# Dealing the first period's work by hand, and spreading two rows' statistics over the tail

## The chip, the cores and the metric

One core of a Trainium2 chip runs the whole program. The metric is the device time of one execution in microseconds (us), median over several executions on the chip. The core has five engines that run side by side, each through its own instructions in order: TensorE (PE in the profile; PEld is its weight load), VectorE (DVE), ScalarE (ACT), GpSimd (POOL) and SyncE (SP, which issues most transfers here).

## The reference, cut to what matters

Two graph layers over 32 batches of 512 nodes with 512 features in float32, each followed by a residual sum and a layer norm. Layer 0 adds over the neighbours. Layer 1 is attention with 8 heads, masked by the same adjacency.

```python
# layer 0:  out = deg * (x @ Wi.T + b) + adj @ (x @ Wj.T)
x = layernorm(x + layer0(x, adj, W, b))
# layer 1:  q, k, v from x; scores masked where adj == 0; softmax; @ v; @ Wo.T + bo
x = layernorm(x + layer1(x, adj, Wq, bq, Wk, bk, Wv, bv, Wo, bo))
```

## The kernel before: the parts that matter here

The batches form a software pipeline. Period n does the attention of batch n-1, and between its matmuls the rest of layer 0 and the projections of batch n, the output projection of batch n-2, and the start of batch n+1. A list of small jobs (`todo`) is dealt to eight steps by estimated cost. The loop takes the steps two at a time, so a period is four double steps, and each of them begins with attention work:

```python
for step in range(0, STEPS, size):            # size 2, in the last period 1
    g, kc = divmod(step, NC)
    for i in range(2):
        scores(b, 2 * g + i, kc)              # PE, then the exponentials on ACT, in place
    for f in due:
        values(*f)                            # PE: the double step before
    for i in range(2):
        mask(2 * g + i, kc)                   # DVE: exponentials times edges
    todo = [f for todo in PERIODS[n][step:step + size] for f in todo]
    while todo and todo[0][1] is between:
        run(todo.pop(0))                      # jobs put between masks and next scores
    ...                                       # row sums of a finished group
    for i in range(2):
        scores(b, 2 * g + i, kc + 1)          # needs the buffers that the masks have read
    ...
    for f in todo: ...                        # the other jobs, masks and sums of kc + 1 among them
```

A layer norm is four kinds of job. `stats` takes two rows of 128 nodes each (a "half"):

```python
def ln_stats(mv, y):
    nc.vector.bn_stats(st, y); nc.vector.bn_aggr(mv[:, 0:2], st)           # DVE
    nc.gpsimd.tensor_scalar(...); nc.gpsimd.tensor_tensor(..., OP.pow); nc.gpsimd.tensor_scalar(...)  # POOL, 128x1
def ln_apply(mv, y):
    nc.scalar.activation(y, y, AF.Identity, bias=mv[:, 4:5], scale=mv[:, 3:4])  # ACT
def l0_norm(b, ic, bank=None):
    ...  # four PE transposes of the applied row into PSUM, ACT copies the result to HT
```

In the first period with attention (n = 1) the jobs stand in this order: six layer-0 pieces with the statistics of half 1 before the last of them, apply half 1, statistics and apply of half 0, two transposed blocks, then query, key and value pieces, then the start of batch 2.

```python
for n in range(1, B):
    todo = phase_b(n) + phase_c(n) + phase_a(n + 1)
    if n < B - 1:
        half = sum(f[0] for f in todo) / 2
    PERIODS += [by_steps(todo, half)]         # cuts by cost: statistics cost 0.0
```

## Time and profile before

| what | us | where it is read |
|---|---|---|
| time, median of the first three runs | 3657.97 | the runs |
| span of the profiled run | 3656.2 | page |
| TensorE busy | 3625.8 | page, part 1 |
| TensorE idle in period 1 | 9.4 | busy time by stretch |
| TensorE's clock in period 1's second double step | 0.85 | the same |

The kernel is bound by TensorE at 99%. A reader should ask where the other 30 us are, since a change of order can win only these and what matmuls lose at a lowered clock. Nearly ten of them are in one period of thirty-two. Here are TensorE's largest waits from 100 us on, summed by kind (total, times, longest), four of eight lines; the prediction shows them in place.

```profile
PE mmb L362 <- ACT xh L305: 5.2, 1, 5.2
PE sc L490 <- DVE e L499: 2.4, 2, 1.7
PE mma L362 <- ACT xh L305: 1.8, 1, 1.8
PE mmb L436 <- DVE k L474: 1.5, 1, 1.5
```

L362 is the transposed block, L305 the apply, L490 the scores, L499 the mask, L436 a matmul of a projection, L474 an addition that moves a projection's result out of PSUM (the memory, in banks, that matmuls write to; a bank is free again when its result has been moved out, which is called its evacuation here). A releaser called "issue" means that the profile shows nothing that was waited for. The first and third line are the second double step, the fourth is the last one; the 1.7 of the second line is in the tail.

### The profile page before, as it was taken

How to read it: one execution, taken by the hardware profiler on the slowest of the kernel's cores; microseconds unless marked ns; L12 is line 12 of the kernel's file. 1: busy time of each engine (PE TensorE's matmuls, PEld its weight loads, DVE VectorE, ACT ScalarE, POOL GpSimd, SP SyncE). 2: the span in 40 equal slices, each digit the busy share in tenths (PEclk: the TensorE clock that was granted, in tenths of full speed). 3: DMA queues.
4: the chain of work that ended last, by engine and by line, in shares of the span. 5: the costliest groups of instructions: out<-in, count | busy, mean ns of one | idle time of the engine just before them, and what ended most of it. 6: DMA issues, size and time to landing. Idle time of an engine off the chain costs nothing.

```text
span 3656.2 us, 49768 instructions
## 1 busy us (share of the span) xinstructions
PE 3625.8 (99%) x18470; PEld 2527.7 (69%) x18470; DVE 2369.8 (65%) x3133; ACT 1035.5 (28%) x1485; POOL 2003.7 (55%) x1984
## 2 busy tenths in 40 slices
PE   9999999999999999999999999999999999999998
PEld 6676777677767766776677667767776777677763
DVE  4566766666666666666666566666666766666665
ACT  2222322222322223222222232232222322222322
POOL 3456455565556565465655555654656456565543
PEclk9999999999999999999999999999999999999999
DMA  8344555545554555555455545555455555445541
GB/s 259 119 127 138 145 161 149 134 140 144 160 159 124 143 145 145 165 148 132 135 149 157 159 121 147 145 153 159 138 140 138 147 162 153 130 137 147 160 133 53
DMA packets 797174, 530.02 MB, mean 145 GB/s; under 512 B 530432, under 2 KB 611840, under 8 KB 796928
## 3 DMA queue, kind: packets, MB, share of 16 engines
q1 hardware_dynamic: 780384, 494.78, 49.1%
q10 hardware_dynamic: 16320, 31.46, 2.5%
q8 instruction: 150, 2.46, 0.3%
q14 instruction: 96, 0.79, 0.1%
q0 software_dynamic: 224, 0.53, 0.0%
HBM read 453.25 MB, written 73.40 MB: 144 GB/s over the span
## 4 chain that ended last, share of the span: by engine, by line
PE 97%; DVE 1%; POOL 1%; issue 0%; ACT 0%; DMA 0%; SPq 0%; DVEq 0%; POOLq 0%
PE mma L436 31%; PE mmb L436 31%; PE sc L490 13%; PE ov L516 12%; PE mmb L334 4%; PE mma L334 3%; PE sc L526 2%; PE mmb L607 0%; PE mma L607 0%; DVE e L499 0%; POOL es L505 0%; DVE es L507 0%; DVE rl L535 0%; PE sc L735 0%; DMA big<-in_adj_dram 0%
## 5 line engine op out<-in xcount | busy, mean ns | idle before, releaser
L499 DVE TENSOR_TENSOR e<-sc,edge 128x1024 f32<-128x1024 f32 x512 | 607.5, 1217 | 493.2 <-PE ov L516 479.6
L494 ACT ACTIVATE sc<-sc 128x1024 f32<-128x1024 f32 x512 | 495.3, 1007 | 922.7 <-PE sc L490 920.2
L436 PE MATMUL mmb<-ring,big 128*128 128x256 f32 x3144 | 730.0, 381 | 0.0
L436 PE MATMUL mma<-ring,big 128*128 128x256 f32 x3112 | 721.3, 380 | 0.7 <-DVE v L465 0.7
L436 PEld LDWEIGHTS mmb<-ring,big 128*128 128x128 f32 x3144 | 595.9, 190 | 104.2 <-issue 24.3
L436 PEld LDWEIGHTS mma<-ring,big 128*128 128x128 f32 x3112 | 588.4, 190 | 105.3 <-issue 22.5
L405 POOL TENSOR_TENSOR big<-big 128x512 f32<-128x512 f32 x376 | 489.1, 1326 | 258.0 <-PE sc L490 234.4
L490 PE MATMUL sc<-q,k 64*128 64x512 f32 x2048 | 513.9, 620 | 2.5 <-DVE e L499 2.4
L516 PE MATMUL ov<-e,v 128*32 128x512 f32 x4096 | 466.8, 595 | 1.2 <-DVE oT L544 1.2
L204 POOL TENSOR_TENSOR xlo<-xh,xhi 128x512 fp32r<-128x512 f32 x128 | 162.2, 1278 | 526.8 <-ACT xhi L203 526.8
L436 PE MATMUL mma<-big,ring 128*128 128x256 f32 x1808 | 429.3, 380 | 0.8 <-issue 0.8
L436 PE MATMUL mmb<-big,ring 128*128 128x256 f32 x1776 | 421.3, 380 | 1.5 <-DVE k L474 1.5
L436 PEld LDWEIGHTS mma<-big,ring 128*128 128x128 f32 x1808 | 342.1, 190 | 62.0 <-issue 14.1
L436 PEld LDWEIGHTS mmb<-big,ring 128*128 128x128 f32 x1776 | 335.6, 190 | 60.9 <-issue 12.2
L490 PEld LDWEIGHTS sc<-q,k 64*128 64x128 f32 x2048 | 165.5, 185 | 287.7 <-DVE e L499 145.8
L300 POOL TENSOR_SCALAR mv<-mv 128x1 f32<-128x1 f32 x256 | 79.8, 312 | 512.4 <-DVE mv L299 500.0
L516 PEld LDWEIGHTS ov<-e,v 128*32 128x32 f32 x4096 | 119.8, 109 | 328.5 <-issue 325.3
L505 POOL TENSOR_TENSOR es<-e 128x1024 f32<-128x1024 f32 x128 | 300.0, 2355 | 77.4 <-DVE e L499 77.4
L507 DVE TENSOR_TENSOR es<-es,e 128x1024 f32<-128x1024 f32 x250 | 300.7, 1224 | 0.0
L451 POOL TENSOR_TENSOR xh<-xh,p 128x512 f32<-128x512 f32 x186 | 230.6, 1268 | 110.3 <-ACT p L443 110.3
L349 POOL TENSOR_TENSOR big<-big,deg_r 128x512 f32<-128x512 f32 x124 | 212.1, 1710 | 76.4 <-DVE big L348 76.4
L454 DVE TENSOR_TENSOR xh<-xh,mma 128x512 f32<-128x512 f32 x186 | 126.9, 682 | 191.2 <-PE mma L436 174.6
(163 smaller groups left out, 3544.0 us busy)
## 6 DMA issues: line engine op xcount, KB each, us to landing
ring<-wo SPq DMA_DIRECT2D x217, 256.0 KB, 2.9
ring<-wq SPq DMA_DIRECT2D x160, 256.0 KB, 3.7
ring<-wv SPq DMA_DIRECT2D x160, 256.0 KB, 3.2
ring<-wk SPq DMA_DIRECT2D x160, 256.0 KB, 4.4
ring<-wi SPq DMA_DIRECT2D x155, 256.0 KB, 2.6
ring<-wj SPq DMA_DIRECT2D x155, 256.0 KB, 2.6
xh<-in_x_dram SPq DMA_DIRECT2D x32, 1024.0 KB, 6.2
xa<-in_x_dram SPq DMA_DIRECT2D x124, 256.0 KB, 4.3
```

The costliest lines, as they stand in the source:

```text
L204: nc.gpsimd.tensor_sub(lo, xs, hi.bitcast(FT))
L334: nc.tensor.matmul(pm, parts[w][:, jc, :], adjR[:, jc, :], start=(w == 0 and jc == 0), stop=(w == 1 and jc == NC - 1))
L349: nc.gpsimd.tensor_tensor(XD[b][:, dc, :], XD[b][:, dc, :], deg_r, op=OP.mult)
L405: nc.gpsimd.tensor_tensor(dst, p, q, op=OP.subtract)
L436: nc.tensor.matmul(pm[:, c * Q:(c + 1) * Q], lhs, rhs, start=first, stop=(kc == 1 and n == len(terms) - 1), skip_group_check=True)
L451: nc.gpsimd.tensor_tensor(d, d, p1, op=OP.add)
L490: nc.tensor.matmul(ps[:, s, :], KT[b, hp // 2][r, hp % 2, kc * P:(kc + 1) * P], QT[b, hp // 2][r, hp % 2, :], start=True, stop=True)
L494: nc.scalar.activation(ps, ps, AF.Exp, scale=QSCALE)
L499: nc.vector.tensor_tensor(e, ps, edge[:, kc:kc + 1, :].to_broadcast([P, 2, N]), op=OP.mult)
L505: nc.gpsimd.tensor_add(ES[i], E[i, 0], E[i, 1])
L507: nc.vector.tensor_add(ES[i], ES[i], E[i, kc])
L516: nc.tensor.matmul(PV[g][r][32 * h:32 * h + 32, :], V[b][:, kc, c0:c0 + 32], E[h // 2, kc][:, h % 2, :], start=(kc == 0), stop=(kc == NC - 1))
```

## The change

The intent: in period 1 the four cuts are set by hand. Layer 0 with all its statistics and applies goes to the first double step, the transposed blocks and the first-half pieces to the second, the rest of the projections to the third, the start of batch 2 to the fourth. In the tail, the statistics of batch 30's four rows are taken two in one step and two in the next.

```diff
@@ last_steps
-                [p[3]], [p[4]], [own[0], z(stats, m, 0), z(stats, m, 1)], [own[1], z(apply, m, 0), z(apply, m, 1), z(store, m)], []]
+                [p[3]], [p[4]], [own[0], z(stats, m, 0)], [own[1], z(apply, m, 0), z(stats, m, 1)], [z(apply, m, 1), z(store, m)]]
@@ for n in range(1, B):
+        if n == 1:
+            a, b, c = [todo.index(f) for f in ((TR, l0_norm, 1, 0, banks(1)[0]), pc("k", 1, 2, banks(1)[0]), phase_a(2)[0])]
+            PERIODS += [[todo[:a], [], todo[a:b], [], todo[b:c], [], todo[c:], []]]
+            continue
```

## The prediction

> **What bounds the kernel now.** I read the page first (busy shares, slices), then PE's waits, then the timelines of the two stretches that the diff touches, then busy time by stretch.
>
> ```profile
> PE 3625.8 (99%) x18470; PEld 2527.7 (69%) x18470; DVE 2369.8 (65%) x3133; ACT 1035.5 (28%) x1485; POOL 2003.7 (55%) x1984
> ```
>
> TensorE is busy 3625.8 of 3656.2 us, so 30.4 us is all the idle time there is. The change adds and removes no matmul: it can win only that idle time, and what matmuls lose at a lower clock. The start (no matmul before 4.04 us, small gaps after) and the end (last matmul at 3649.0, program end at 3656.2) hold about half of it, and neither is touched. The rest lies in period 1 (106.49 to 217.13 us: attention of batch 0, projections of batch 1, start of batch 2) and in the tail. By stretch (length, then PE busy; the clock follows POOL's column), the four double steps of period 1, and then period 2, which is the steady state:
>
> ```profile
> 106.49:131.44 24.95, 24.95 (x114) 19.46 (x113) 10.66 (x15) 3.85 (x4) 20.29 (x19) 1.00 0.42 123
> 131.44:164.86 33.42, 26.39 (x129) 18.11 (x129) 15.16 (x20) 12.94 (x20) 9.40 (x12) 0.85 0.31 95
> 164.86:191.84 26.98, 26.13 (x138) 17.51 (x137) 16.19 (x22) 6.82 (x10) 7.58 (x5) 1.00 0.69 185
> 191.84:217.13 25.29, 23.80 (x121) 15.69 (x121) 20.86 (x22) 6.71 (x9) 13.59 (x10) 1.00 0.25 75
> 217.13:329.30 112.17, 112.17 (x577) 78.95 (x576) 73.73 (x97) 32.10 (x46) 63.01 (x63) 1.00 0.52 146
> ```
>
> Period 2 has no idle time at all, so whatever period 1 saves moves everything after it earlier. The second double step has 7.03 us idle and a mean clock of 0.85: (1 - 0.85) / (1 - 0.5) x 33.42, some 10 us at half rate. The timeline of it:
>
> ```profile
> 136.92 2.03 PE L490 MATMUL sc<-q,k 64*128 64x512 f32 x8
> 144.16 1.12 PE L362 MATMUL mmb<-ident,xh 128*128 128x128 f32 x4 [5.21 <-ACT xh L305]
> 147.10 1.12 PE L362 MATMUL mma<-ident,xh 128*128 128x128 f32 x4 [1.83 <-ACT xh L305]
> 148.01 3.62 PE L436 MATMUL mmb<-ring,big 128*128 128x256 f32 x8
> ...
> 177.74 1.97 PE L436 MATMUL mma<-big,ring 128*128 128x256 f32 x8 [0.85 <-issue]
> ...
> 210.03 1.99 PE L436 MATMUL mmb<-big,ring 128*128 128x256 f32 x8 [1.49 <-DVE k L474]
> ```
>
> The transposes of batch 1 wait for the normalised rows; afterwards eight matmuls take 3.62 us that take 1.89 elsewhere. Why the rows are late is on VectorE:
>
> ```profile
> 137.69 2.35 DVE L507 TENSOR_TENSOR es<-es,e 128x1024 f32<-128x1024 f32 x2
> 139.95 1.21 DVE L499 TENSOR_TENSOR e<-sc,edge 128x1024 f32<-128x1024 f32 x1
> 141.09 0.68 DVE L298 BATCH_NORM_STATS2 st<-xh 128x6 f32<-128x512 f32 x1
> ```
>
> The sum of the last layer-0 piece was done at 132.3, but the statistics of half 0 were dealt to the second double step, behind two masks, two sums of exponentials and a third mask: 8.8 us later.
>
> **What the Trainium skill says.** (1) "TensorE: Matmul & The Clock Gate", Part 1: the array runs at half clock after an idle window of about 3.4 us and needs a busy one to recover; the windows run freely. The trace agrees: the 5.21 us gap is followed by about 10 us at half rate, while gaps of 1.49 and 1.69 us are not. (2) The same page, "Architectural detail": ScalarE's and VectorE's queues are strict FIFO. The trace agrees: the two applies of half 1, ready at 132.3 (GpSimd's last operation for them), ran at 139.92, behind four exponentials. (3) "SBUF — State Buffer", "Who interferes with whom": a VectorE instruction with two SBUF inputs and a GpSimd one that reads SBUF exclude each other. The trace agrees: a 0.26 us GpSimd scalar operation took 1.94 at 144.26, beside a sum of exponentials on VectorE. This is why the second row came 2.95 us after the first.
>
> **The change, part by part: period 1.** The loop takes steps in pairs, so the four non-empty lists are the four double steps. The order of pieces is kept; only the cuts move.
>
> Stage 1 keeps its six layer-0 pieces, 24.95 us, and gains at its end apply (half 1), statistics and apply (half 0). VectorE starts the latter at 132.2 instead of 141.09 and ends 1.7 later, at 133.9; GpSimd makes three small operations a row (1.2 us), ending at 134.4 and 135.65; ScalarE applies the rows (0.8 each), ending at 135.2 and 136.5.
>
> Stage 2 then has scores, values, scores (7.44 us: 191.84 to 199.28 is the same), four transposed blocks (1.74; eight transposes took 0.87 at 155.19), five pieces (8.7, at 1.73 each): 17.9 us. Two waits are new. The first exponentials now stand behind the applies: 136.45 instead of 132.61. The first ends at 137.45, its mask (1.22) at 138.7, and only then may the next scores reuse that buffer; PE would have been ready at 136.92. That is 1.8, and 0.1 for the second buffer. The transposes follow at 140.8 with no wait, but their copies on ScalarE (0.56) stand behind the next two exponentials, which end at 142.0; the first value piece starts at about 142.55 instead of 141.7: 0.85. Stage 2 is 17.9 + 1.95 + 0.85 = 20.7 us.
>
> Stage 3: scores, values, row sums, scores (8.31, as 164.86 to 173.17) and eleven pieces (19.1): 27.4. The 0.85 "issue" of before is, by my reading, a bank wait: the evacuation that frees it stood behind four reciprocals and two products (VectorE 172.09 to 176.86). Now the last first-half key piece, evacuated by ScalarE, stands in front. The reciprocals end about 12.0 after the stage's start; the first query evacuation ends at 12.9, and the piece that needs it is due at 13.5: no wait.
>
> Stage 4 becomes exactly what it is in period 2, 302.22 to 329.32: 27.10 us, no idle time. The 1.49 disappears with the shifted cut.
>
> Sum: 24.95 + 20.7 + 27.4 + 27.1 = 100.15 against 110.64: 10.5. I take 10.3, as neither new wait can be trusted to a tenth.
>
> **The tail.** Matmul, VectorE and GpSimd:
>
> ```profile
> 3627.23 1.13 PE L490 MATMUL sc<-q,k 64*128 64x512 f32 x4 [1.69 <-DVE e L499]
> ...
> 3625.95 2.36 DVE L499 TENSOR_TENSOR e<-sc,edge 128x1024 f32<-128x1024 f32 x2 [3.72 <-POOL es L505]
> ...
> 3622.43 0.19 POOL L300 TENSOR_SCALAR mv<-mv 128x1 f32<-128x1 f32 x1
> 3622.70 0.55 POOL L301 TENSOR_TENSOR mv<-mv,mhalf 128x1 f32<-128x1 f32 x1
> 3623.36 0.26 POOL L302 TENSOR_SCALAR mv<-mv 128x1 f32<-128x1 f32 x1
> 3623.58 2.34 POOL L505 TENSOR_TENSOR es<-e 128x1024 f32<-128x1024 f32 x1
> ```
>
> Scores waited for a mask, the mask for a buffer that a GpSimd sum reads, and that sum stood behind the small operations of four rows. Two rows move a step later: 2 x 1.27 = 2.5 us off this chain. The sum ends at 3623.4, the mask at 3624.7, and PE needs the buffer at 3625.4: the whole 1.69 goes, plus 0.2 of restart, 1.9. The moved statistics run at 3624.7 to 3626.3 on VectorE, before the next mask can start (its exponential ends at 3626.6). The moved applies lie behind the last exponentials, and end about 3629.2, before ScalarE's row-sum drain, due 3632.6. The store goes out 4.5 us later, still over 20 us before the end. I count 1.8.
>
> Together 12.1: 3657.97 - 12.1 = 3645.9.
>
> **Rivals.** *The clock falls again.* The waits of 1.8 and 0.85 lie 4 us apart with transposes between; if they count as an idle window, the half rate returns and costs about what it did: 10.3 lost in that stage less 7.04 idle is 3.3. For: the windows' thresholds are not in the trace. Against: gaps of 1.69 left the clock alone. It makes 3649. *The exponentials behind the applies cost more than I say*, or the evacuations in stage 3 block: 1 to 3 us, 3647 to 3649. For: ScalarE's and VectorE's queues are in order, and more is now put in front of them. *The gain is hidden anyway*, because weight loads or layer-0 input for batch 2 now arrive late: 3656. Against: the ring is seven tiles deep with 3 us loads, and batch 2's first use is now about 17 us after its load is issued, instead of 11. *The tail gains nothing*, if another operand holds the mask: 3648.
>
> **Range and chances.** Repeats of before span 2.1 us. The best case is both new waits overlapped, 3643; the rivals that I believe end at 3649 to 3650. So 3643 to 3650 at 8 in 10. A 2% change is 73 us, over twice all idle time, and nothing here can lose as much: within 2% at 0.98.
>
> **What would show it.** Right: no lowered clock between 106 and 217 us; period 1 about 100 us; the 5.21 and 1.83 us waits replaced by one near 1.8 us of the scores for a mask and one under 1 us of the value piece for the transposed copy; no wait in stages 3 and 4; in the tail no wait over a microsecond for a mask. Wrong: a half-rate stretch still there, a new wait over 3 us in stage 2 or 3, or a mask still released by GpSimd's sum.

## The result, and the profile after

The change takes 3646.07 us (3644.95 to 3648.8, six runs) against 3658.1 (3657.25 to 3659.63, six runs). The ratio is 0.9968, with an interval of 0.9955 to 0.998. A ratio here is the mean time of one kernel's fast runs over that of the other's of the same rounds, so it is not quite the ratio of the medians. Run a second time in a later experiment, beside another set of runs of before, the change had 3646.33 us and 0.997.

In the profile taken with these runs TensorE is busy for 3624.8 us, 1.0 less than before:

```profile
PE 3624.8 (99%) x18470; PEld 2526.2 (69%) x18470; DVE 2370.0 (65%) x3133; ACT 1036.1 (28%) x1485; POOL 2004.7 (55%) x1984
```

The four double steps of period 1 in that profile (length, then busy time of PE, PEld, DVE, ACT, POOL; then the granted clock):

```profile
108.68:133.63 24.95, 24.95 (x113) 19.45 (x113) 10.67 (x15) 4.24 (x5) 20.31 (x19) 1.00 0.42 125
133.63:155.82 22.19, 20.05 (x105) 12.15 (x104) 14.41 (x18) 11.09 (x16) 5.33 (x11) 0.92 0.25 68
155.82:183.32 27.50, 27.50 (x145) 19.12 (x144) 16.48 (x23) 7.39 (x12) 9.61 (x6) 1.00 0.70 204
183.32:210.43 27.11, 27.11 (x138) 18.80 (x137) 20.93 (x23) 7.82 (x11) 14.03 (x10) 1.00 0.44 111
```

The first, third and fourth are as the prediction has them, full to the end. The second has 2.1 us idle, and its clock is 0.92, not 1: the fall that the prediction hoped to be rid of is shorter, but there. In the second profile of the change (the later experiment) the other three have the same lengths, and this one differs:

```profile
131.26:152.39 21.13, 18.61 (x105) 11.45 (x104) 14.41 (x18) 11.01 (x16) 5.33 (x11) 1.00 0.23 67
```

The clock stayed, and the stretch is 1.06 us shorter. TensorE's timeline there, first in the first profile, then in the second (start, length, instruction, and in brackets the idle time before it):

```profile
141.12 3.21 PE L490 MATMUL sc<-q,k 64*128 64x512 f32 x8 [1.93 <-DVE e L499]
144.26 1.11 PE L362 MATMUL mmb<-ident,xh 128*128 128x128 f32 x4
```

```profile
138.75 2.26 PE L490 MATMUL sc<-q,k 64*128 64x512 f32 x8 [1.93 <-DVE e L499]
140.94 0.65 PE L362 MATMUL mmb<-ident,xh 128*128 128x128 f32 x4
141.43 0.60 PE L362 MATMUL mma<-ident,xh 128*128 128x128 f32 x4
142.62 1.99 PE L436 MATMUL mmb<-ring,big 128*128 128x256 f32 x8 [0.59 <-ACT big L363]
```

Both have the same new wait of 1.93 us. In the first, the scores after it take 3.21 us, in the second 2.26. The second also shows the other new wait, 0.59 us of the first value piece for the copy (L363).

In the tail, the scores of the last step start without a wait: the sum on GpSimd stands behind two rows, not four, and the mask that it releases is early enough. PE, DVE and POOL in the first profile:

```profile
3617.52 1.99 PE L490 MATMUL sc<-q,k 64*128 64x512 f32 x8
...
3616.58 1.23 DVE L499 TENSOR_TENSOR e<-sc,edge 128x1024 f32<-128x1024 f32 x1 [1.24 <-POOL es L505]
...
3614.16 2.38 POOL L505 TENSOR_TENSOR es<-e 128x1024 f32<-128x1024 f32 x1
```

The account, before against the second profile of the change (spans 3656.16 and 3644.10 us):

| part | before | change | difference |
|---|---|---|---|
| start to the first scores | 106.49 | 106.31 | -0.2 |
| period 1 | 110.64 | 100.69 | -9.95 |
| periods 2 to 31 | 3352.1 | 3352.0 | -0.1 |
| period 32 and tail, to the start of the last matmul | 79.49 | 77.53 | -1.96 |
| start of the last matmul to the end | 7.4 | 7.5 | +0.1 |

The gain is not idle time alone. TensorE's busy time is 3625.8 us before and 3622.3 in this profile, so 3.5 of the 12.06 us between the spans are matmul time. In period 1 the busy time fell by 3.1 us (101.27 to 98.17, the sums over the four double steps) and the idle time by 6.85 (9.37 to 2.52). That fits the clock, as an estimate: before, TensorE worked for 6.06 of the 10.24 us at half rate, which loses half of that, 3.0 us.

In the first profile the start took 108.68 us, 2.2 more, in code that the change doesn't touch; it is the slowest of its six runs (3648.8). The trace shows both parts of it. The first transposes waited 6.8 us for the adjacency, in the second profile 5.5. And TensorE was busy 1.07 us longer up to the first scores: the first clock record at full rate is at 19.0 us, in the second profile at 15.4, and four matmuls that began at 17.34 took 1.86 us where four like them take 1.08 later. With the window at half rate (1.44 us of busy time) this is why the page above hides the gain in busy time.

### The profile page after: what moved, and what is told of

Same layout as the page of the kernel before. It is cut to its first block, busy times and chain, and to the rows that moved or that the text cites.

```text
span 3647.0 us, 49766 instructions
## 1 busy us (share of the span) xinstructions
PE 3624.8 (99%) x18470; PEld 2526.2 (69%) x18470; DVE 2370.0 (65%) x3133; ACT 1036.1 (28%) x1485; POOL 2004.7 (55%) x1984
## 4 chain that ended last, share of the span: by engine, by line
PE 98%; DVE 1%; POOL 0%; ACT 0%; DMA 0%; issue 0%; SPq 0%; DVEq 0%; POOLq 0%
PE mma L436 31%; PE mmb L436 31%; PE sc L490 13%; PE ov L516 12%; PE mmb L334 4%; PE mma L334 3%; PE sc L526 2%; PE mmb L607 0%; PE mma L607 0%; DVE rl L535 0%; DMA big<-in_adj_dram 0%; PE sc L735 0%; DVE e L499 0%; POOL es L505 0%; POOL big L405 0%
## 5 line engine op out<-in xcount | busy, mean ns | idle before, releaser
L436 PEld LDWEIGHTS mma<-big,ring 128*128 128x128 f32 x1808 | 341.7, 190 | 60.0 <-issue 12.1
L454 DVE TENSOR_TENSOR xh<-xh,mmb 128x512 f32<-128x512 f32 x186 | 127.0, 683 | 190.6 <-PE mmb L436 174.2
```

The lines of the kernel that those rows point to most:

```text
L436: nc.tensor.matmul(pm[:, c * Q:(c + 1) * Q], lhs, rhs, start=first, stop=(kc == 1 and n == len(terms) - 1), skip_group_check=True)
L454: nc.vector.tensor_tensor(d, d, pm, op=OP.add)
```

## The experiments

Ten variants and the change once more ran, each with five timed rounds and beside the kernel before; all were correct. Intervals of the ratios are about 0.0013 to either side, 5 us, so for the small parts the lengths of stretches in the traces carry the verdict, one profile each.

**Period 1 alone** (the change, with the tail of before).

```diff
-                ... [own[0], z(stats, m, 0)], [own[1], z(apply, m, 0), z(stats, m, 1)], [z(apply, m, 1), z(store, m)]]
+                ... [own[0], z(stats, m, 0), z(stats, m, 1)], [own[1], z(apply, m, 0), z(apply, m, 1), z(store, m)], []]
```

> The change's deal of period 1 with the tail of the kernel before. My theory: the two parts add up, period 1 wins about 10 us and the tail about 2, so this run is near 3648 us (3646.5 to 3649.5), ratio to before 0.9973. In its profile the tail's 1.69 us wait of the scores for a mask is back. Rival: part of the gain of period 1 comes only together with the tail, or the tail is worth 3 us or more: then this run is at 3649.5 or above. It also gives one more sample of the clock in period 1: the profile of the whole change showed one stretch of 3.4 us at half rate there; if that depends on where the free-running window falls, it may be missing here, and period 1 then takes about 100 us instead of 101.75.

Measured: 3649.36 us (3647.34 to 3649.72) against 3658.3, ratio 0.9976. Period 1 took 100.69 us, the clock stayed, and in the tail the wait of 1.71 us is back. As expected, at the upper edge.

**The tail alone** (before, with the change's tail; the same lines the other way round).

> The change's tail with the period 1 of the kernel before. Theory: the 1.69 us wait of the scores for the mask goes, and with its restart the tail is 1.9 us shorter: 3656.2 us, ratio 0.9995. Rival: the wait is hidden behind something else at the end (row sums, store), and the time stays at 3658.1; or the traces' difference of the tail, 2.3 us, is all real, 3655.8.

Measured: 3656.8 us (3656.6 to 3657.69) against 3658.3, ratio 0.9997 with an interval that holds 1. In the trace the wait is gone and the stretch from the last period's start to the last matmul is 77.52 us, before 79.49: 1.97 us. The first theory's size is right; that the 2.3 us of the first pair of traces is all real falls, as the rest lies after the last matmul, where the two profiles of the change differ by 0.4 us. The medians of the two parts, 8.9 and 1.5 us, add to 10.4 of some 12. By the traces, 9.95 and 1.97 add to 11.9. The times alone can't tell these apart.

**Only the first cut.**

```diff
+            half = sum(f[0] for f in todo) / 2
+            was = by_steps(todo, half)
+            b, c = [sum(len(s) for s in was[:i]) for i in (4, 6)]
             PERIODS += [[todo[:a], [], todo[a:b], [], todo[b:c], [], todo[c:], []]]
```

(and the tail of before)

> Only the first cut of period 1 is moved (statistics and applies of half 0 go to the end of the first double step); the two later cuts fall where the kernel before has them, and the tail is that of before. Theory: the second double step loses its 5.21 and 1.83 us waits and about 10 us at half rate, and gains a wait near 1.9: about 7.5 us gained. The waits of the third and fourth double step (0.85 and 1.49, with their restarts 2.6) stay, so this is some 2.5 us above the run of period 1 alone: about 3650.5 us. Rival: those two waits were only followers of the late second double step and vanish with it; then this equals the run of period 1 alone, and the hand-made later cuts are worth nothing.

Measured: 3652.31 us (3649.41 to 3653.07), ratio 0.9981; 2.95 us above period 1 alone by the medians, expected 2.5. The times of the two overlap (the lowest here are 3649.41 and 3649.59, the highest there is 3649.72), so the trace decides. TensorE's waits in period 1, the three longest:

```profile
PE sc L490 <- DVE e L499: 1.9, 1, 1.9
PE mmb L436 <- DVE k L474: 1.5, 1, 1.5
PE mma L436 <- issue: 0.9, 1, 0.9
```

The two later waits are exactly where they were, so they belong to the later cuts and did not follow from the late second double step. Which of the two cuts removes which wait was not separated. The third and fourth double step take 26.98 and 25.31 us, as in the kernel before. In this profile the clock fell for one window of 3.4 us, as in the first profile of the change; period 1 took 104.85 us, 3.1 above that one's 101.75.

**The gap filled with useless work** (before, plus matmuls into the bank that the block overwrites).

```diff
         pt = mm_tile(bank) if bank else turn_tile()
+        if b == 1 and ic == 0:
+            for i in range(18):
+                nc.tensor.matmul(pt, adjR[:, 0, 0:P], adjR[:, i % NC, :], start=True, stop=True)
```

> The kernel before, with 18 useless matmuls (0.23 us each, 4.2 us) in front of the first transposed block of batch 1, into the bank that the block then overwrites: they fill most of the 5.21 us in which TensorE waits. They take nothing away from what it waits for. Theory: the idle window is what halves the clock; filled, the clock stays whole, the transposes and the first value piece run at full rate, and the kernel gets about 3 us FASTER for doing more work: 3655 us, ratio 0.9991. Rival: the slow matmuls after the gap come from something else (late operands, the transposes): then the time is as before, 3658, or longer, and the matmuls after the gap still take 3.6 us for eight.

Measured: 3657.38 us (3656.13 to 3659.59), ratio 0.9998. By the signs the rival came true: the time is as before, and in the profile the eight matmuls after the gap still take 3.62 us. But the profiled run is the slowest of five, and its timeline says why:

```profile
145.14 0.65 PE L365 MATMUL mmb<-ident,xh 128*128 128x128 f32 x4 [0.91 <-ACT xh L305]
148.08 1.12 PE L365 MATMUL mma<-ident,xh 128*128 128x128 f32 x4 [2.29 <-ACT xh L305]
```

The first wait shrank, the first block ran at full rate (0.65 in place of 1.12), and the second wait, now 2.29, let the clock fall instead. It was at half for 6.83 us, not 10.24. The mean clock that is listed with every run points the same way: it is 0.998 in the two slowest of the five (3659.27 and 3659.59 us), as in every run of before, and 0.999 in the other three (3656.13 to 3657.38). So the experiment was too small, and it was repeated:

**Both gaps filled** (22 and 8 matmuls).

```diff
+        if b == 1 and ic < 2:
+            for i in range((22, 8)[ic]):
+                ...                        # the matmul of the run before
```

> The kernel before with useless matmuls in both waits: 22 (5.1 us) in front of the first transposed block, 8 (1.85 us) in front of the second. The run with the first wait filled alone left 2.29 us idle in the second, and in its profile the clock still fell, later, for 6.8 us. Theory: with no window of 3.4 us more than half idle, the clock does not fall at all; the second double step takes about 30.3 us in place of 33.4, and the kernel about 3655 us. Rival: useless matmuls do not keep the clock up, or the slow stretch was not the clock: the second double step stays at 33.4 or above.

Measured: 3655.7 us (3655.22 to 3656.25) against 3658.18 (3656.99 to 3659.08); no times of the two overlap in these rounds, though the ratio's interval (0.998 to 1.0008) holds 1. The mean clock is 0.999 in all five runs and 0.998 in all nine of before. The second double step:

```profile
131.29:162.38 31.09, 30.64 (x159) 21.36 (x158) 15.16 (x20) 12.95 (x20) 9.39 (x12) 1.00 0.34 108
```

The kernel does 30 matmuls more and is 2.3 us faster in this stretch (33.42 to 31.09), at a clock of 1.00. The half rate after the wait is thus shown to be a cost of its own, caused by the idleness and not by what TensorE was waiting for. It was worth 2.3 us, not the 3.3 of the prediction (the first expectation had 3). Part of the difference shows in the traces: the slow first block (1.12 us, here 0.66) cost nothing, because the second one, which waits for GpSimd's second row, began 15.66 us into the stretch before and 15.67 us here.

**The applies between masks and scores** (the change, with the applies of half 0 put off).

```diff
-        ... z(stats, n, 0), z(apply, n, 0), (TR, l0_norm, n, 0, A), (TR, l0_norm, n, 1, K)]
+        ... z(stats, n, 0), z(between, apply, n, 0), (TR, l0_norm, n, 0, A), (TR, l0_norm, n, 1, K)]
```

(and the cut before that job)

> The whole change, but the two applies of half 0 are issued in the second double step between its masks and its second pair of scores, so that ScalarE does the first pair of exponentials before them. Theory: the 1.93 us wait of the scores for a mask comes from the exponentials standing behind these applies in ScalarE's in-order queue. Without it the masks start about 3 us earlier, the wait is gone, no window is idle enough to halve the clock; what remains is 0.9 us in which the first value piece waits for the transposed copy. About 2.0 to 3.0 us below the change: 3643.5 us. Rival: the wait is for the buffer of the masked exponentials (freed by the value matmuls), not for ScalarE: then nothing changes, 3646.

Measured: 3642.95 us (3641.8 to 3644.03), ratio 0.996, against 3646.33 (3645.86 to 3648.3) for the change in the same rounds. ScalarE's queue in the change shows what this took away:

```profile
136.75 0.81 ACT L305 ACTIVATE xh<-xh,mv 128x512 f32<-128x512 f32 x1 [1.42 <-POOL mv L302]
138.03 0.81 ACT L305 ACTIVATE xh<-xh,mv 128x512 f32<-128x512 f32 x1 [0.46 <-POOL mv L302]
138.75 1.91 ACT L494 ACTIVATE sc<-sc 128x1024 f32<-128x1024 f32 x2
```

The scores of these exponentials began at 133.63. The exponentials waited until 138.75 behind these two rows, which waited for GpSimd. With the applies behind them the 1.93 us wait is gone, and the second double step takes 18.91 us, 2.2 less. What remains is 0.61 us of the first value piece. The rival (the wait is for the buffer of the masked exponentials) falls.

**The transposed blocks between as well.** The two blocks after that apply are made `z(between, l0_norm, ...)` too.

> As the run before, and the first two transposed blocks of batch 1 also go between the masks and the second pair of scores. Theory: they are ready (rows applied about 1 us before TensorE gets there or just then), their copies stand in front of the second pair of exponentials, and no wait is left in period 1: it takes about 97.5 to 98 us, and the kernel is at 3642.5 us, some 3.5 below the change. Rival: the transposes now wait for the applies, which come late behind the first exponentials, and the exponentials behind the copies delay the masks: then it is no better than the run with the applies alone.

Measured: 3642.62 us (3642.04 to 3642.77), ratio 0.9958; no run of the change in the same rounds is below 3645.86. Not one wait of TensorE is left in the second double step:

```profile
131.06:149.26 18.20, 18.20 (x105) 11.54 (x104) 15.57 (x18) 10.91 (x16) 5.33 (x10) 1.00 0.29 78
```

Period 1 takes 97.78 us. This version beats both kernels in these rounds, by 3.7 us (the change) and 15.5 us (before). Between it and the run with the applies alone the traces differ by 0.7 us in period 1; their times overlap.

**The change again** (no edit), in the rounds of the two variants above.

> The change itself once more, beside the two variants on the same chip. Theory: 3646 us, with a spread of 2 to 4 us from run to run, larger than that of the kernel before, because the wait of 1.9 us is at the edge of what the clock's window counts as idle: in some runs one window of 3.4 us at half rate, in others none. Rival: the spread is of the start of the kernel, which is the same in both; then the spread of this and of the kernel before are alike.

Measured: 3646.33 us (3645.86 to 3648.3), ratio 0.997, against 3658.11 (3656.15 to 3658.94). The spread is 2.4 us, that of before in the same rounds 2.8: they are alike, as the rival has it. That the clock falls in some executions and not in others is shown by the two profiles (0.92 and 1.00 in the second double step); that this makes the spread is not.

**The wait filled in the change** (5 useless matmuls where it waits 1.93 us).

```diff
+    def fill():
+        pt = mm_tile("b")
+        for i in range(5):
+            nc.tensor.matmul(pt, adjR[:, 0, 0:P], adjR[:, i % NC, :], start=True, stop=True)
-        ... z(apply, n, 0), (TR, l0_norm, n, 0, A), ...
+        ... z(apply, n, 0), z(between, fill), (TR, l0_norm, n, 0, A), ...
```

(and the cut before that job)

> The whole change, with 5 useless matmuls (1.15 us) between the masks and the second pair of scores of the second double step, where the change waits 1.93 us. In four profiles the clock fell where that wait lay within one window of 3.4 us (56 and 57% idle) and not where it was split between two (41 and 30%). Theory: with 0.8 us left idle it never falls; the wait itself ends no earlier, so the second double step takes 21.14 us in every run, and the times lie at the lower end of those of the change, about 3645.5 us, none above 3647.5. Rival: the fall has to do with something else than idle time; then some runs still show it, and the times spread as those of the change, up to 3648.

Measured: 3646.08 us (3645.07 to 3647.44). In the profile the clock stayed and the second double step took 21.12 us, as predicted, but one profile can't show that it never falls. None is above 3647.5, yet the median, expected near 3645.5, is that of the change, and the times still spread over 2.4 us. So this run too gives no sign that the clock's fall in period 1 makes the spread. The profiles point to the start: in twelve profiles of kernels with the same code up to there, the first scores begin between 104.75 and 107.46 us, and in the thirteenth, the first of the change, at 108.68. In the earliest of them (104.75, the applies between) the clock was first recorded at full rate at 10.7 us, in the latest at 19.0. So the moment when the clock comes up at the start moves with it; how much of the spread of the times this makes was not tested.

**All four rows one step later** (before, with another tail).

```diff
-  ... [own[0], z(stats, m, 0), z(stats, m, 1)], [own[1], z(apply, m, 0), z(apply, m, 1), z(store, m)], []]
+  ... [own[0]], [own[1], z(stats, m, 0), z(stats, m, 1), z(apply, m, 0), z(apply, m, 1), z(store, m)], []]
```

> The kernel before, with the statistics of all four rows moved one step later in the tail, where their applies are (instead of two and two). Theory: what costs is that the second sum of exponentials on GpSimd stands behind the small operations of rows that nobody waits for; moving all four takes the sum to the front, and the 1.69 us wait goes as in the run of the tail alone: 3656.2 us. VectorE then has four rows (3.3 us) in front of the last masks, 1.3 us more than their exponentials take, still before the last values need them. Rival: two at a time is needed, since four rows in front of the last masks delay the values of the last step: 3657 to 3658.

Measured: 3663.99 us (3661.87 to 3664.51) against 3658.11: 6 us lost, which neither theory had. The wait of the scores is gone, as expected; a new one of 4.20 us stands before the row sums, and the clock fell after it. ScalarE in the last steps:

```profile
3629.28 0.81 ACT L305 ACTIVATE xh<-xh,mv 128x512 f32<-128x512 f32 x1 [0.46 <-POOL mv L302]
3630.55 0.81 ACT L305 ACTIVATE xh<-xh,mv 128x512 f32<-128x512 f32 x1 [0.46 <-POOL mv L302]
3631.27 1.00 ACT L494 ACTIVATE sc<-sc 128x1024 f32<-128x1024 f32 x1
```

The last exponentials stand behind four applies, each of which waits for GpSimd, 1.27 us a row; their scores began at 3625.63. A new theory: it is ScalarE's queue, as in period 1, and not the number of rows.

**All four rows later, with the applies in the last step.**

```diff
+  ... [own[0]], [own[1], z(stats, m, 0), z(stats, m, 1)], [z(apply, m, 0), z(apply, m, 1), z(store, m)]]
```

> The kernel before with all four statistics one step later in the tail, as in the run that lost 6 us, but with the four applies and the store in the last step, so that the last exponentials stand in front of the applies in ScalarE's queue. Theory: what that run lost was ScalarE, whose last exponentials stood behind applies that waited for GpSimd, not the four rows on VectorE; put right, this equals the run of the tail alone: 3656.7 us, the tail from the last period's start to the last matmul 77.5 us as against 79.5. Rival: four rows in front of the last masks on VectorE are too many, and TensorE waits 1 us or more for the last masks: 3657.5 or above.

Measured: 3656.36 us (3653.63 to 3657.48), and 77.52 us from the last period's start to the last matmul, the same as with the tail alone. So "two at a time" is not what matters in the tail: the second sum on GpSimd must not stand behind all four rows (behind two, in the change, it is early enough), and the last exponentials must not stand behind the four applies. The change meets both.

## Why the prediction was right, and where it was off

**The bound.** Only idle time and lost clock were to be won, and both were: between the spans of before and of the second profile about 8.5 us of idle time and 3.5 us of busy time. The time fell by 12.03 us, predicted 12.1. Periods 2 to 31 passed the gain through (difference 0.1 us), so the rival that it is hidden later falls.

**First double step.** 24.95 us, exactly as said.

**Second double step.** Predicted 20.7, measured 21.13 with the clock whole and 22.19 with one window at half. The terms: its work without a wait is 18.2 (the version with no wait), said to be 17.9; the wait behind the applies is 1.93, said 1.8 plus 0.1 (the prediction's own sum puts in 1.95 for these); the copy costs 0.59, said 0.85. The mechanism of the first wait is shown by the run with the applies between, that of the copy by the one with the blocks between.

**The clock.** The step that failed is the statement that no lowered clock would be left, with the argument that gaps of 1.69 us did not lower it. A gap of 1.93 us can. The fall cost 1.06 us in the first profile, and was absent in the second. The argument was weak in itself: the clock moves in windows (last section), and in the trace of before the gap of 1.69 lay across two of them, so that neither was idle for more than 38%. The prediction had the fall as a rival, at 3.3 us. Its reading of the cause in the kernel before, idleness, is shown by the run with both gaps filled; its size there is 2.3 us.

**Third and fourth double step.** 27.5 and 27.1, predicted 27.4 and 27.1. In the third, the query evacuation ended 12.95 us after the start and the piece that needs it began at 13.6, said 12.9 and 13.5. That both old waits belong to the later cuts is shown by the run with the first cut only. That the 0.85 "issue" is a wait for the bank is only argued: before, the evacuation of it ended at 177.64 and the piece began at 177.74.

**The sum.** Period 1 was to take 100.15 us: 100.69 and 101.75. So it won 9.95 and 8.89 us where 10.3 was counted: taking 10.3 in place of 10.5 was right in direction and too little.

**The tail.** Counted at 1.8, worked out as 1.9, and it is 1.97 in the trace. The chain (scores, mask, sum on GpSimd, small operations of four rows) is shown by two other tails that take the rows out of it. The gain in the times, 1.5 us, is within noise. That these rows could have moved together, if the applies moved too, was not seen before.

**Overall.** The midpoint agrees to 0.2 us, which is partly luck: run to run the change moves by nearly 4 us, two of which lie in the untouched start.

## What to carry to other kernels

When one engine is busy 99% of the time, list its remaining waits and ask in which in-order queue the thing it waits for stands behind something that nobody needs yet; moving a job across that point adds no work. Then ask the same of the jobs moved: here the applies, moved forward, stood in front of exponentials, and putting them one place later won another 3 us. A wait of TensorE near two microseconds is worth removing even when its length seems not to matter, because the clock can fall after it, as it did in one of the change's two profiles.

## What the Trainium skill lacked or had wrong

- "TensorE: Matmul & The Clock Gate", Part 1, says the clock falls after an idle window. Here a window did not have to be idle: the clock records change in steps of 3.413 us, and laying that grid over TensorE's timeline gives the idle share of the window before a change. The clock fell after windows idle for 57% (1.93 us, the change) and 56% (1.92, only the first cut), and for 84% and 67% (before, the gap filled). It stayed after 49% (1.68 us, in the tail of the run with the gap filled), 44% (1.49, before, last double step of period 1) and 41% (1.41, the change's second profile). After the last long stretch of work, at the program's end, it also fell after windows idle for 53% (both gaps filled, and all four rows later). So the border lies between 49 and 53%; that it is one half is a guess.
- The same part: because the windows run freely, the same wait of 1.93 us lowered the clock in one profile of the change and not in the other, where it was split between two windows (nor with period 1 alone: split into 30 and 26%). The page tells this of the warm-up only.
- The same part says that a busy window brings the clock back. With the gap filled, a window at half rate that was 27% idle (147.15 to 150.57) did not, and the next one did. But another 0.91 us of it were transposes. If these don't count as busy, it was 54% idle, and the border may be the same as above; no run here separates the two.
- The same page, "Architectural detail", has the queues of ScalarE and VectorE as in order. The traces agree: in the change the exponentials, whose scores began at 133.63, started at 138.75, behind the applies. No page draws the consequence: a job that waits for a slow chain (1.27 us a row on GpSimd) blocks what stands behind it, 4.20 us of TensorE's time in one tail.
- "SBUF — State Buffer", "Who interferes with whom", agrees: in the kernel before a GpSimd operation of 0.26 us took 1.94 beside a VectorE sum of two SBUF inputs; in the change, with VectorE idle there, the same operation took 0.27.
